# Where the last image's gathers, stores and loads stand in the order of a four-layer hybrid kernel

## The chip, the cores and the metric

The kernel runs on one core of a Trainium2 chip, in one launch. The metric is the device time of the whole kernel in microseconds, the median of several runs. The engines are named as in the profile: PE is the matrix engine, DVE the vector engine, ACT the scalar engine, POOL the general engine, and SP the engine that here issues nearly all DMAs. Each engine works through its own instructions in the order in which they were issued to it and waits on semaphores for what the others produce. SP does so too: a DMA issue that has to wait holds up every issue behind it.

## The reference

Four images of 32 x 32 positions with 256 channels (1024 tokens each) pass four layers. Cut to what matters:

```python
# layer 0: ln -> w_in -> 3x3 depthwise conv -> gelu -> selective scan, 512 channels, 64 states
h = dA * h + (dtt * xt)[:, :, None] * Bt[:, None, :]        # 1024 steps
y = einsum('bdn,bn->bd', h, Ct)                             # ... + skip, ln, w_out, residual
# layer 1: grouped convolutions; layer 2: masked attention and a mixture of 8 experts
# layer 3: selective scan, 512 channels, 16 states
dt = softplus(x_conv @ W_dt + b_dt)
y_t = (h_new * C_t[:, None, :]).sum(-1)                     # ... * silu(gate) @ W_out, residual
# layer 3's mixture: every token is given to its two best of 8 experts
h = gelu(xf @ w1[e] + bb1[e]); y = h @ w2[e] + bb2[e]; out = out + cw[:, e:e+1] * y
```

## The kernel before

**Scans.** There are eight selective scans, one for each image of layer 0 and of layer 3, in the order `SCANS` = (0,0), (0,1), (3,0), (0,2), (3,1), (0,3), (3,2), (3,3). Each is cut into units of 128 pairs of channel and state by 1024 steps: 256 units for a scan of layer 0, 64 for one of layer 3, 1280 in all. For one unit SP loads `dA<-dt` (512 KB, line 501, four units ahead, five buffers), ACT takes the exponential, PE spreads the input's three bf16 parts over the states (`ps_rep`), DVE multiplies by the rows of B and runs the scan instruction, POOL multiplies `h` by the rows of C, and PE sums the states (`ps_y`). The outputs go by ACT (`yo`) and SP (line 552) to memory and are read back (`y_back`, line 924).

**Ticks.** All other work is written as generators (`front`, `middle` and `last` for each image), and one step of a generator is a tick. `run()` issues, after each half of a unit, up to `TICKS` = 2 ticks, and only while no engine's planned clock is ahead of the vector engine's. So the order on every engine is fixed when the kernel is built: units and ticks woven together. `pipe(items, step1, step2, ...)` is a software pipeline: in one tick it issues the last step of an old item first and the first step of the newest last. `need()` forces ticks where a scan's inputs are not yet made; a new chunk of parts may be late by `LATEST` = 5 units. `beside(main, other)` alternates the ticks of two generators; `some(other, n)` takes n ticks of another; `until(name, b)` yields empty ticks until a mark is set in `passed`, while the order is made.

**Startup.** `prepare()` runs the preparation parts one after the other; the last, `prepare_moe`, clears 4 MB of memory for the piles with 15 stores of 256 KB (line 1616) over five ticks. `front(1)` follows, which loads image 1 (line 791, 1 MB), takes its layer norm (`ln_st`), and puts it through `w_in` and the depthwise convolution (`inward`).

**Layer 3's front.** `front3` makes a scan's inputs. `steps` computes dt and its product with the input, and splits that in three bf16 parts: `project` (PE, then ACT's softplus), `add` (DVE, POOL), `split` (stores dt, line 698; ACT casts part 0; DVE takes the remainder; ACT casts part 1), `low` (part 2), `store` (line 713). For image 3 (`last`) the first two items are done ahead, with `BETWEEN` = 8 ticks of image 2's piles in between (`self.other`), and the later items alternate with those piles.

**Experts.** `piles` does layer 3's mixture for one image. Its tokens have been scattered by expert (POOL, indirect DMA) into 15 piles of 256 rows. Items go through a pipeline: `t` loads a pile's rows (`fetch`, line 1909) and turns them on PE (`ps_gx`) with a copy by ACT; two `h` items multiply by W1 with a gelu; an `o` item multiplies by W2 (`ps_e`), and a copy `x` (ACT for image 2, DVE for image 3, `lone`) is stored to `results` (line 1974). `layer(0, t)` and `layer(1, t)` load W1 and W2 of a pile's expert (line 1915), two buffers each. Rows have `many` buffers: 3 for image 2, 8 for image 3. At the end `gather` brings back each token's two rows (POOL, indirect DMA, `rows_m<-results,slot`), `add` adds them with their shares (DVE, `tb_rows`), and the image goes out (line 2009). Image 2's piles lie beside scan (3,3), the last one; image 3's come after all scans.

Almost all engine instructions are recorded at line 135, that of a helper, so the views are read by tile names.

Of the kernel before, what the change touches and what calls it, by code (L numbers as in the profile page):

```python
# [9 lines left out]
F32 = mybir.dt.float32  # L10
BF16 = mybir.dt.bfloat16
# [7 lines left out]
P = 128  # L19
NB = 4  # L20
L = 1024
TB = L // P
C = 256
# [6 lines left out]
FEW = 256  # L30
PILES = (2 * L + NEXP * (FEW - 1)) // FEW
# [18 lines left out]
BETWEEN = 8  # L50
# [93 lines left out]
END = object()  # L144


class Hybrid:
# [503 lines left out]

    def steps(self, fp, key, w, src, chunks, bias, u, between=None):


        nc = self.nc
# [5 lines left out]
        def tile2(tag, bufs):  # L663
            return fp.tile([P, 512], F32, tag="sp_" + tag, name="sp_" + tag, bufs=bufs)

        def linear(item):
            d, g = item
            ps = self.ps("ps_dt")
            self.mm(ps, lambda k: w(k, d), src, chunks, slice(g * 512, (g + 1) * 512))

            r, e, l = (tile2(t, n) for t, n in (("r", 3), ("e", 2), ("l", 3)))
            nc.scalar.activation(r, ps, AF.Relu, bias=bias[:, d : d + 1])
            nc.scalar.activation(e, ps, AF.Abs, bias=bias[:, d : d + 1])
            got[item] = r, e, ps, l
# [17 lines left out]
            by.tensor_tensor(r, l, r, ALU.add)  # L692
            by.tensor_tensor(l, r, u[:, d, g * 512 : (g + 1) * 512], ALU.mult)

        def split(item):
            d, g = item
            r, _, _, x = got[item]
            nc.sync.dma_start(self.mem["dt", *key, d][:, g * 512 : (g + 1) * 512], r)
            X = fp.tile([P, 3, 512], BF16, tag="parts", name="parts", bufs=3)
            rest = tile2("x", 2)  # L700
            nc.scalar.copy(X[:, 0, :], x)
            nc.vector.tensor_tensor(rest, x, X[:, 0, :], ALU.subtract)
            nc.scalar.copy(X[:, 1, :], rest)
            got[item] = rest, X

        def low(item, by=nc.gpsimd):
            rest, X = got[item]
# [12 lines left out]
        if between is not None:  # L720
# [16 lines left out]
            self.parts_direct(range(1), nc.scalar)  # L737
            self.ready.add(("parts", *key, 0))
            yield 3.0
        yield from self.pipe(items, project, add, split, low, store, cost=3.0)  # L740

# [33 lines left out]
    def front(self, b):  # L777
# [3 lines left out]
        with tc.tile_pool(name=f"f{b}", bufs=1, side="right") as op:  # L781
# [4 lines left out]
            with tc.tile_pool(name=f"fa{b}", bufs=1, side="right") as fp:  # L786
# [9 lines left out]
                pads = [fp.tile([P, 34, 34], F32, name=f"pad{i}") for i in range(2 + len(vector))]  # L796
                for pad in pads:
                    nc.gpsimd.memset(pad, 0.0)
                yield 1.0
                xT = fp.tile([P, 2, L], F32, name="xT0")  # L800
                if b:
# [22 lines left out]

                def inward(item):
                    d, g, k = item
                    pad = pads[2 + vector.index(d) if d in vector else d % 2]
                    if g < 0:
                        h = k
# [752 lines left out]
    def prepare_moe(self, st):  # L1582

        nc, a = self.nc, self.a
        self.router, self.b2, raws = {}, {}, {}
        for which, router, b2 in (
            (2, "L2_ffn_router_w", "L2_ffn_b2"), (3, "L3_ffn_gate_w", "L3_ffn_b2")
        ):
            wr = self.const.tile([P, 2, NEXP], F32, name=f"wr{which}")
            if a[router].shape[0] == NEXP:  # L1590
                raws[which] = st.tile([NEXP, C], F32, name=f"raw{which}")
                nc.sync.dma_start(raws[which], a[router])
            else:
                nc.sync.dma_start(wr, a[router].rearrange("(k p) e -> p k e", p=P))
            self.router[which] = wr
            self.b2[which] = self.const.tile([NEXP, C], F32, name=f"b2{which}")
            nc.sync.dma_start(self.b2[which], a[b2])
        self.gb = self.const.tile([P, NEXP], F32, name="gb")
        nc.sync.dma_start(
            self.gb, a["L3_ffn_gate_b"].rearrange("(o e) -> o e", o=1).to_broadcast([P, NEXP])  # L1600
        )
        self.bout3 = self.rows("L3_attn_b_out")
        self.earlier = self.const.tile([P, P], BF16, name="earlier")
        make_upper_triangular(nc, self.earlier, diag=False)
        count = st.tile([P, PILES], I32, name="counti")
        nc.gpsimd.iota(count, pattern=[[1, PILES]], base=0, channel_multiplier=0)
        self.count = self.const.tile([P, PILES], F32, name="count")
        self.one8 = self.const.tile([P, NEXP], F32, name="one8")
        zeros = st.tile([P, 2, C], F32, name="zeros")
        nc.gpsimd.memset(zeros, 0.0)  # L1610
        self.piled = self.keep(("piled",), [PILES * FEW, C])
        yield
        nc.vector.tensor_copy(self.count, count)
        nc.vector.memset(self.one8, 1.0)
        for t in range(PILES):
            nc.sync.dma_start(self.pile(self.piled, t), zeros)
            if t % 3 == 2:
                yield
        for which, raw in raws.items():
            ps = self.ps("ps_r", (P, C))  # L1620
            for k in range(2):
                nc.tensor.transpose(
                    ps[:, k * NEXP : (k + 1) * NEXP], raw[:, k * P : (k + 1) * P],
                    self.ident[:NEXP, :NEXP],
                )
            nc.vector.tensor_copy(
                self.router[which].rearrange("p k e -> p (k e)"), ps[:, : 2 * NEXP]
            )
# [267 lines left out]
    def piles(self, op, b, tb, picks, slot, share, whose, bias):  # L1896
# [2 lines left out]
        w1, w2 = self.a["L3_ffn_W1"], self.a["L3_ffn_W2"]  # L1899
        results = self.keep(("results", b), [PILES * FEW, C])  # L1900
        lone = b == NB - 1
        many = 8 if lone else 3
        reuse = self.x0.rearrange("p (k j) c -> p k j c", k=4)
        rows, weights, turned, hidden, got = {}, {}, {}, {}, {}

# [14 lines left out]
        def one(item):  # L1920
            kind, t, i = item
            if kind == "t":
                x = rows.pop(t)
                got[item] = ps = self.ps("ps_gx", (P, 2, FEW))
                for c in range(2):
# [24 lines left out]
        def two(item):  # L1950
# [7 lines left out]
            elif kind == "h":  # L1958
                ps = got.pop(item)
                for k in range(2):  # L1960
# [1 line left out]
                    nc.scalar.activation(  # L1962
                        hidden[t][:, f, :], ps[:, k, :], AF.Gelu, bias=bias[:, t, f : f + 1]
                    )
                if i == 1:
                    layer(0, t + 2)
            else:
                y = reuse[:, 2 + t % 2]
                ps = got.pop(item)
# [1 line left out]
                    nc.vector.tensor_copy(y, ps)  # L1971
                else:
                    nc.scalar.copy(y, ps)
                nc.sync.dma_start(self.pile(results, t), y)
                layer(1, t + 2)

        items = []
# [11 lines left out]
        for t in range(2):  # L1989
            fetch(t)  # L1990
        yield 0.5
        yield from self.pipe(items, one, two, cost=2.0)

        def gather(j):
            got[j] = x = op.tile([P, 2, C], F32, tag="rows", name="rows_m", bufs=many)
# [12 lines left out]
                )  # L2008
            nc.sync.dma_start(self.image(self.out, b)[:, j, :], tb[:, j, :])

        yield from self.pipe(range(TB), gather, lambda j: None, add, cost=2.0)

    def route(self, gp, lg, cw, renorm, spots=None):

# [53 lines left out]
    def front3(self, b, tb):  # L2068
# [3 lines left out]
        with tc.tile_pool(name=f"g{b}", bufs=1, side="right") as op:  # L2072
# [76 lines left out]
            with tc.tile_pool(name=f"gc{b}", bufs=1, side="right") as fp:  # L2149
# [6 lines left out]
                def low(g):  # L2156
# [2 lines left out]
                    self.mm(ps[: 2 * N, :], lambda k: w_bc[:, k, :], u, DC, cols)  # L2159
                    nc.scalar.activation(bct[:, cols], ps[: 2 * N, :], AF.Identity, bias=bbc)  # L2160

                yield from self.pipe(range(2), low, cost=3.4)
                nc.sync.dma_start(self.keep(("bc", *key), [2 * N, L]), bct)
                steps = self.steps(
                    fp, key, lambda k, d: w_dt[:, k, d * P : (d + 1) * P], u, DC,
                    vec["L3_attn_b_dt"], u, self.some(self.other, BETWEEN) if last else None,
                )
                if last:
                    steps = self.beside(steps, self.other, lambda: ("parts", *key, 0) in self.ready)
# [107 lines left out]
    def prepare(self):  # L2277
        with self.tc.tile_pool(name="prepb", bufs=1, side="right") as st:
# [6 lines left out]
                yield 0.5  # L2285
            for part in parts:
                for _ in part:
                    yield 1.0
                yield 3.0

    def middle(self, b):
# [56 lines left out]

    def last(self, b):
        if b == NB - 2:  # L2350
            self.other, before = self.ahead(b + 1, "right"), self.other
            yield from self.beside(before, self.other)
            return
        if b == NB - 1:
            for more in self.other:
                if more is not END:
                    yield more
            return
        with self.tc.tile_pool(name=f"e{b}", bufs=1, side="right") as tp:
            tb = tp.tile([P, TB, C], F32, name="tb")  # L2360
# [47 lines left out]
```

## Time and profile before

| | us |
|---|---|
| median of 3 runs (lowest to highest) | 6268.16 (6258.17 to 6272.56) |
| the profiled execution | 6287.39 |
| its span | 6285.6 |
| DVE busy | 5033.5 (80%) |
| PE busy | 4983.6 (79%) |
| POOL busy | 3891.1 (62%) |
| ACT busy | 3391.2 (54%) |

The profile is of one execution, on one core. The span is from the first recorded instruction to the last; 1.8 us of the execution lie around it. The page gives each engine's busy time and the span in 40 equal slices, where a digit is the busy share in tenths and one slice is 157 us. `PEclk` is the granted clock of the matrix engine (mean 0.823). A line of the timeline gives start, duration, engine, line, operation and tiles, the number of instructions drawn together, and in brackets the engine's idle time before it with what ended it. A line of the waits gives who waited for what, the sum, the count and the longest. A row of the windows gives, for one stretch, the busy time of each engine with its instructions, the granted clock, the mean busy share of the 16 DMA engines and GB/s.

### The profile page before, as it was taken

How to read it: one execution, taken by the hardware profiler on the slowest of the kernel's cores; microseconds unless marked ns; L12 is line 12 of the kernel's file. 1: busy time of each engine (PE TensorE's matmuls, PEld its weight loads, DVE VectorE, ACT ScalarE, POOL GpSimd, SP SyncE). 2: the span in 40 equal slices, each digit the busy share in tenths (PEclk: the TensorE clock that was granted, in tenths of full speed). 3: DMA queues.
4: the chain of work that ended last, by engine and by line, in shares of the span. 5: the costliest groups of instructions: out<-in, count | busy, mean ns of one | idle time of the engine just before them, and what ended most of it. 6: DMA issues, size and time to landing. Idle time of an engine off the chain costs nothing. (4 is left out here: it accounts for less than half of the span.)

```text
span 6285.6 us, 59857 instructions
## 1 busy us (share of the span) xinstructions
PE 4983.6 (79%) x19881; PEld 2042.3 (32%) x19881; DVE 5033.5 (80%) x3977; ACT 3391.2 (54%) x4329; POOL 3891.1 (62%) x2016
## 2 busy tenths in 40 slices
PE   5686776579898567979869978979769969996757
PEld 2121221032243112225324532234225432453436
DVE  5889898998898998889899988889889984224661
ACT  3465665345577434649647735558637734425622
POOL 2787768665576866568676766568767754114551
PEclk7686786589899658979869988979869979998868
DMA  3554555544345556435555576345555673025945
GB/s 108 180 155 161 164 176 181 174 147 129 116 161 179 189 160 165 141 121 173 175 191 166 182 181 166 125 131 185 161 183 176 186 183 96 12 70 150 246 109 171
DMA packets 382814, 977.72 MB, mean 156 GB/s; under 512 B 40644, under 2 KB 149520, under 8 KB 380880
## 3 DMA queue, kind: packets, MB, share of 16 engines
q1 hardware_dynamic: 376704, 962.73, 50.8%
q0 software_dynamic: 5200, 10.53, 0.6%
q8 instruction: 163, 2.67, 0.2%
q14 instruction: 171, 1.40, 0.1%
q10 hardware_dynamic: 576, 0.39, 0.0%
HBM read 867.76 MB, written 108.36 MB: 155 GB/s over the span
## 5 line engine op out<-in xcount | busy, mean ns | idle before, releaser
L135 POOL TENSOR_TENSOR h<-h,rows 128x1024 f32<-128x1024 f32 x1280 | 3025.0, 2367 | 1706.8 <-DVE h L135 1324.9
L135 DVE TENSOR_TENSOR_SCAN h<-dA,ps_rep 128x1024 f32<-128x1024 f32 x1280 | 2924.4, 2285 | 212.7 <-ACT dA L135 82.2
L135 DVE TENSOR_TENSOR ps_rep<-ps_rep,rows 128x1024 f32<-128x1024 f32 x1280 | 1549.3, 1210 | 189.6 <-PE ps_rep L135 188.3
L135 PE MATMUL ps_rep<-S,spread_L_conv_A_log 96*128 96x512 bf16 x2048 | 753.4, 457 | 778.8 <-DVE h L135 733.2
L135 ACT ACTIVATE dA<-dA,A_L_conv_A_log 128x1024 f32<-128x1024 f32 x1024 | 1125.7, 1142 | 440.3 <-DMA dA<-dt 405.3
L135 PE MATMUL ps_y<-h,collect_L_conv_A_log 128*32 128x512 f32 x4096 | 706.6, 745 | 17.2 <-POOL h L135 17.2
L135 PEld LDWEIGHTS <-spread_L_conv_A_log 96*128 96x128 bf16 x2048 | 160.0, 103 | 1566.9 <-DVE h L135 1272.8
L135 PE MATMUL ps_e<-we,h_m 128*128 128x256 f32 x2528 | 587.7, 383 | 5.5 <-ACT h_m L135 5.5
L135 ACT ACT_TABLE_LOAD x395 | 506.8, 1283 | 30.9 <-DMA dA<-dt 14.7
L135 PEld LDWEIGHTS ps_e<-we,h_m 128*128 128x128 f32 x2528 | 478.8, 191 | 129.6 <-ACT h_m L135 25.8
L135 PE MATMUL ps_h<-xTm,we 128*128 128x512 f32 x1024 | 487.9, 607 | 0.1
L135 ACT ACTIVATE p<-ps_sc 128x512 f32<-128x512 f32 x404 | 219.3, 594 | 331.6 <-PE ps_sc L135 327.7
L135 ACT ACTIVATE dA<-dA,A_L_attn_A_log 128x1024 f32<-128x1024 f32 x256 | 284.3, 1144 | 194.7 <-DMA dA<-dt 162.1
L135 PE MATMUL ps_rep<-S,spread_L_attn_A_log 96*128 96x512 bf16 x512 | 182.0, 443 | 194.0 <-DVE h L135 171.8
L135 PE MATMUL ps_at<-p,v 128*32 128x512 f32 x1024 | 275.0, 617 | 0.2 <-ACT p L135 0.2
L135 PE MATMUL ps_at<-p,ones 128*32 128x512 f32 x1024 | 275.0, 617 | 0.0
L135 ACT ACTIVATE h_m<-ps_h,cols 128x512 f32<-128x512 f32 x256 | 171.0, 686 | 186.8 <-PE ps_h L135 185.0
L135 PEld LDWEIGHTS ps_h<-xTm,we 128*128 128x128 f32 x1024 | 192.4, 193 | 218.7 <-issue 154.1
L135 PE MATMUL ps_sc<-qT,kT 32*128 32x512 f32 x808 | 249.0, 666 | 5.9 <-ACT p L135 2.0
L135 PE MATMUL ps_cv<-pad,diag 128*128 128x512 f32 x504 | 231.0, 599 | 0.0
L135 PEld LDWEIGHTS ps_y<-h,collect_L_conv_A_log 128*32 128x32 f32 x4096 | 93.7, 118 | 339.5 <-issue 227.7
L135 POOL TENSOR_TENSOR tb<-tb,y_m 128x512 f32<-128x512 f32 x160 | 202.7, 1274 | 0.0
(392 smaller groups left out, 5609.5 us busy)
## 6 DMA issues: line engine op xcount, KB each, us to landing
dA<-dt SPq DMA_DIRECT2D x1280, 512.0 KB
we<-in_L_ffn_W_dram SPq DMA_DIRECT2D x92, 512.0 KB
parts<-parts SPq DMA_DIRECT2D x60, 384.0 KB
S<-parts SPq DMA_DIRECT2D x90, 256.0 KB
dt<-sp_r SPq DMA_DIRECT2D x64, 256.0 KB
y<-yo SPq DMA_DIRECT2D x128, 128.0 KB
y_back<-y SPq DMA_DIRECT2D x64, 256.0 KB
we<-in_L_ffn_w_dram SPq DMA_DIRECT2D x64, 256.0 KB
```

The source lines that it names most:

```text
L135: return got(*args, **kw)
```

## The change

Five things are moved or split; what is computed stays the same.

- The memory for the piles is cleared in `front(1)`: one of the 15 stores, from a tile `empty` made there, ahead of each of the first 15 `inward` items. The five ticks in `prepare_moe` go, and the other parts' `yield` in `prepare` becomes `pass` (none of them has a tick left there).
- `piles` has a third step, `three`: the loads of W1 and W2 for pile t+2 and the store of a result are issued one tick later, for both images.
- Image 2's rows have 2 buffers instead of 3; its gathers and adds follow each other without an empty tick.
- Image 2's gathers wait, in the order of issue, until image 3's piles have begun (`turned`, set at the `t` item of pile 1). For that, image 3's `last` also runs what is left of image 2.
- For image 3, `steps` splits the parts in two ticks, `high` and `remainder` (`apart`), with four buffers instead of three for `l` and the parts; and one tick of image 2's piles (its first weights and rows) is taken ahead of the pipe of `low` in `front3`.

```diff
--- before.py
+++ after.py
@@ -651,7 +651,7 @@
-    def steps(self, fp, key, w, src, chunks, bias, u, between=None):
+    def steps(self, fp, key, w, src, chunks, bias, u, between=None, apart=False):
         nc = self.nc
@@ -668,7 +668,7 @@
             ps = self.ps("ps_dt")
             self.mm(ps, lambda k: w(k, d), src, chunks, slice(g * 512, (g + 1) * 512))
-            r, e, l = (tile2(t, n) for t, n in (("r", 3), ("e", 2), ("l", 3)))
+            r, e, l = (tile2(t, n) for t, n in (("r", 3), ("e", 2), ("l", 3 + apart)))
             nc.scalar.activation(r, ps, AF.Relu, bias=bias[:, d : d + 1])
             nc.scalar.activation(e, ps, AF.Abs, bias=bias[:, d : d + 1])
             got[item] = r, e, ps, l
@@ -692,16 +692,24 @@
             by.tensor_tensor(r, l, r, ALU.add)
             by.tensor_tensor(l, r, u[:, d, g * 512 : (g + 1) * 512], ALU.mult)
-        def split(item):
+        def high(item):
             d, g = item
             r, _, _, x = got[item]
             nc.sync.dma_start(self.mem["dt", *key, d][:, g * 512 : (g + 1) * 512], r)
-            X = fp.tile([P, 3, 512], BF16, tag="parts", name="parts", bufs=3)
+            X = fp.tile([P, 3, 512], BF16, tag="parts", name="parts", bufs=3 + apart)
+            nc.scalar.copy(X[:, 0, :], x)
+            got[item] = x, X
+
+        def remainder(item):
+            x, X = got[item]
             rest = tile2("x", 2)
-            nc.scalar.copy(X[:, 0, :], x)
             nc.vector.tensor_tensor(rest, x, X[:, 0, :], ALU.subtract)
             nc.scalar.copy(X[:, 1, :], rest)
             got[item] = rest, X
+
+        def split(item):
+            high(item)
+            remainder(item)
         def low(item, by=nc.gpsimd):
             rest, X = got[item]
@@ -737,7 +745,8 @@
             self.parts_direct(range(1), nc.scalar)
             self.ready.add(("parts", *key, 0))
             yield 3.0
-        yield from self.pipe(items, project, add, split, low, store, cost=3.0)
+        parted = (high, remainder) if apart else (split,)
+        yield from self.pipe(items, project, add, *parted, low, store, cost=3.0)
@@ -796,6 +805,12 @@
                 pads = [fp.tile([P, 34, 34], F32, name=f"pad{i}") for i in range(2 + len(vector))]
                 for pad in pads:
                     nc.gpsimd.memset(pad, 0.0)
+                empty = None
+                if b == 1:
+                    self.piled = self.keep(("piled",), [PILES * FEW, C])
+                    empty = fp.tile([P, 2, C], F32, name="empty")
+                    nc.gpsimd.memset(empty, 0.0)
+                    piles = iter(range(PILES))
                 yield 1.0
                 xT = fp.tile([P, 2, L], F32, name="xT0")
                 if b:
@@ -824,6 +839,8 @@
                 def inward(item):
                     d, g, k = item
+                    if empty is not None and (t := next(piles, None)) is not None:
+                        nc.sync.dma_start(self.pile(self.piled, t), empty)
                     pad = pads[2 + vector.index(d) if d in vector else d % 2]
                     if g < 0:
                         h = k
@@ -1606,16 +1623,9 @@
         nc.gpsimd.iota(count, pattern=[[1, PILES]], base=0, channel_multiplier=0)
         self.count = self.const.tile([P, PILES], F32, name="count")
         self.one8 = self.const.tile([P, NEXP], F32, name="one8")
-        zeros = st.tile([P, 2, C], F32, name="zeros")
-        nc.gpsimd.memset(zeros, 0.0)
-        self.piled = self.keep(("piled",), [PILES * FEW, C])
         yield
         nc.vector.tensor_copy(self.count, count)
         nc.vector.memset(self.one8, 1.0)
-        for t in range(PILES):
-            nc.sync.dma_start(self.pile(self.piled, t), zeros)
-            if t % 3 == 2:
-                yield
         for which, raw in raws.items():
             ps = self.ps("ps_r", (P, C))
             for k in range(2):
@@ -1899,7 +1909,7 @@
         w1, w2 = self.a["L3_ffn_W1"], self.a["L3_ffn_W2"]
         results = self.keep(("results", b), [PILES * FEW, C])
         lone = b == NB - 1
-        many = 8 if lone else 3
+        many = 8 if lone else 2
         reuse = self.x0.rearrange("p (k j) c -> p k j c", k=4)
         rows, weights, turned, hidden, got = {}, {}, {}, {}, {}
@@ -1920,6 +1930,8 @@
         def one(item):
             kind, t, i = item
             if kind == "t":
+                if lone and t == 1:
+                    self.passed.add(("turned", b))
                 x = rows.pop(t)
                 got[item] = ps = self.ps("ps_gx", (P, 2, FEW))
                 for c in range(2):
@@ -1962,8 +1974,6 @@
                     nc.scalar.activation(
                         hidden[t][:, f, :], ps[:, k, :], AF.Gelu, bias=bias[:, t, f : f + 1]
                     )
-                if i == 1:
-                    layer(0, t + 2)
             else:
                 y = reuse[:, 2 + t % 2]
                 ps = got.pop(item)
@@ -1971,7 +1981,14 @@
                     nc.vector.tensor_copy(y, ps)
                 else:
                     nc.scalar.copy(y, ps)
-                nc.sync.dma_start(self.pile(results, t), y)
+                got[item] = y
+
+        def three(item):
+            kind, t, i = item
+            if kind == "h" and i == 1:
+                layer(0, t + 2)
+            if kind == "o":
+                nc.sync.dma_start(self.pile(results, t), got.pop(item))
                 layer(1, t + 2)
         items = []
@@ -1989,7 +2006,9 @@
         for t in range(2):
             fetch(t)
         yield 0.5
-        yield from self.pipe(items, one, two, cost=2.0)
+        yield from self.pipe(items, one, two, three, cost=2.0)
+        if not lone:
+            yield from self.until("turned", NB - 1)
         def gather(j):
             got[j] = x = op.tile([P, 2, C], F32, tag="rows", name="rows_m", bufs=many)
@@ -2008,7 +2027,8 @@
                 )
             nc.sync.dma_start(self.image(self.out, b)[:, j, :], tb[:, j, :])
-        yield from self.pipe(range(TB), gather, lambda j: None, add, cost=2.0)
+        between = (lambda j: None,) if lone else ()
+        yield from self.pipe(range(TB), gather, *between, add, cost=2.0)
     def route(self, gp, lg, cw, renorm, spots=None):
@@ -2159,11 +2179,13 @@
                     self.mm(ps[: 2 * N, :], lambda k: w_bc[:, k, :], u, DC, cols)
                     nc.scalar.activation(bct[:, cols], ps[: 2 * N, :], AF.Identity, bias=bbc)
+                if last:
+                    yield from self.some(self.other, 1)
                 yield from self.pipe(range(2), low, cost=3.4)
                 nc.sync.dma_start(self.keep(("bc", *key), [2 * N, L]), bct)
                 steps = self.steps(
                     fp, key, lambda k, d: w_dt[:, k, d * P : (d + 1) * P], u, DC,
-                    vec["L3_attn_b_dt"], u, self.some(self.other, BETWEEN) if last else None,
+                    vec["L3_attn_b_dt"], u, self.some(self.other, BETWEEN) if last else None, last,
                 )
                 if last:
                     steps = self.beside(steps, self.other, lambda: ("parts", *key, 0) in self.ready)
@@ -2285,7 +2307,7 @@
                 yield 0.5
             for part in parts:
                 for _ in part:
-                    yield 1.0
+                    pass
                 yield 3.0
     def middle(self, b):
@@ -2348,13 +2370,12 @@
     def last(self, b):
         if b == NB - 2:
-            self.other, before = self.ahead(b + 1, "right"), self.other
+            after = self.ahead(b + 1, "right")
+            self.other, before = (more for more in after if more is not END), self.other
             yield from self.beside(before, self.other)
             return
         if b == NB - 1:
-            for more in self.other:
-                if more is not END:
-                    yield more
+            yield from self.other
             return
         with self.tc.tile_pool(name=f"e{b}", bufs=1, side="right") as tp:
             tb = tp.tile([P, TB, C], F32, name="tb")
```

## The prediction

> **What bounds the kernel now.** I read the page's slices first, then busy time by stretch, then the timeline and the waits of the places where the change acts.
>
> ```profile
> span 6285.6 us, 59857 instructions
> ...
> DVE  5889898998898998889899988889889984224661
> ...
> L135 DVE TENSOR_TENSOR_SCAN h<-dA,ps_rep 128x1024 f32<-128x1024 f32 x1280 | 2924.4, 2285 | 212.7 <-ACT dA L135 82.2
> L135 DVE TENSOR_TENSOR ps_rep<-ps_rep,rows 128x1024 f32<-128x1024 f32 x1280 | 1549.3, 1210 | 189.6 <-PE ps_rep L135 188.3
> ```
>
> For 33 of the 40 slices DVE is at 8 or 9 tenths. It does 1280 scan units, each a multiply (1.21 us) and a scan (2.29 us); the timeline repeats them every 3.54 us. Everything else is woven beside them, so up to the last scan only what stops DVE counts. After it (the 4224661) the tail is a chain of its own. The stretches where the change acts:
>
> ```profile
> core 0: us, PE busy (x) PEld busy (x) DVE busy (x) ACT busy (x) POOL busy (x), PEclk, DMA share, GB/s
> 240.00:262.00 22.00, 4.52 (x15) 0.72 (x13) 9.92 (x15) 2.43 (x2) 11.57 (x8) 0.58 0.89 287
> 5720.00:5830.00 110.00, 75.47 (x250) 37.18 (x248) 71.17 (x50) 68.86 (x90) 72.98 (x43) 0.81 0.65 176
> 5830.00:6007.00 177.00, 137.38 (x628) 87.34 (x632) 130.32 (x77) 115.93 (x142) 96.89 (x45) 0.88 1.02 251
> 6007.00:6048.00 41.00, 15.81 (x44) 1.62 (x36) 37.96 (x26) 6.11 (x6) 33.05 (x24) 0.50 0.44 122
> 6130.00:6254.00 124.00, 113.46 (x540) 99.13 (x540) 10.38 (x15) 35.04 (x76) 0.00 (x0) 0.94 0.57 188
> ```
>
> First row, startup: DVE idle more than half the time, DMA nearly full. Second and third, image 3's scan while image 2's expert piles run: DVE idle 39 of 110 and 47 of 177 us, with DMA full (1.02) in the latter. Fourth, the last scans: DVE full, but with the wrong work. Fifth, image 3's own piles: PE bound, DVE and POOL free.
>
> **The change part by part.** The sum is made against the profiled execution (6287.39 us, span 6285.6), 19 us above the median of 6268.16; I take the difference over to the median unchanged.
>
> *Zero rows.*
>
> ```profile
> 236.35 2.15 SPq L1616 DMA_DIRECT2D piled<-zeros  x3
> 239.91 9.96 SPq L1616 DMA_DIRECT2D piled<-zeros  x12
> 253.95 0.42 SPq L791 DMA_DIRECT2D x<-in_x_dram  x1
> 261.37 0.43 DVE L135 BATCH_NORM_STATS2 ln_st<-x 128x6 f32<-128x256 f32 x1 [11.69 <-DMA dA<-dt]
> ```
>
> Fifteen stores (256 KB each, 4 MB) hold SP until 249.9. Behind them queue dA loads and image 1's 1 MB x load, which goes out at 253.95; DVE stands 11.69 us for it (the releaser printed is a dA load, but the statistics read x). The change takes the stores and five ticks out here, so front 1 starts about one unit (3.5 us) earlier in the order, and the x load goes out at about 243 and lands about 7 us later as now (253.95 to 261.37), near 250. DVE gets to the statistics one unit earlier, at about 246, so it stalls some 4 us instead of 11.69: gain 7 (3 to 10, the lower end if dA loads still hold it). The stores come back one for each `inward` item (0.2 to 0.7 us of SP each in the rows above) at about 280 to 340, where the share is 0.50 at 153 GB/s: hidden there at nothing; uncovered they cost 15 x 0.7 = 10. The memset (522 ns on POOL) only moves. The Trainium skill, "DMA: Bandwidth & Descriptors", section "Issuing engines are not separate DMA queues", speaks against a gain: it says that all DMAs share the same 16 engines and interleave, so moved bytes cost what they cost; by it alone 4 MB would only move its 16 us (4 MB at the 251 GB/s above), and the sum would lose these 7. I stay with the share of 0.50.
>
> *Image 3's parts and the early tick.* Five weights and rows (2.5 MB) go out about 30 us sooner, into a stretch with a share of 0.10 (5640 to 5680). First loads now go at 5682.08 and the rows land at 5692.3, but ACT's softplus runs to 5693.25 anyway, so PE starts piles only 0.5 us sooner. The eight ticks between reach one tick further: one 4.8-us o item and a gelu (0.84 + 1.28 of table load). Then PE stands 7.43 us for the first rep, which takes the o item; ACT loses 2 us, under its 11.1-us wait for dA. The waits of 5690 to 5800 show what the split into two ticks is for:
>
> ```profile
> DVE sp_x L135 <- ACT parts L135: 25.2, 6, 6.7
> ACT parts L135 <- DVE sp_x L135: 4.5, 6, 0.8
> ```
>
> DVE, in order, stands 4.2 us six times at the subtract behind ACT's cast, holding its units. With a tick between, the cast is done when the subtract comes: 25 us of this wait go. But the stretch is a loop of ACT and PE (projection 5.2 on PE, then 6.6 on ACT: 11.8 of a cycle of about 12, from the relu times 5744.1, 5756.6, 5768.6, 5780.5, 5794.5), so what comes next for DVE is ps_rep or dA; only ACT's own 4.5 us and no more leave the loop. The added tick makes the second parts ready later, against a limit of 5 units: a forced tick, 0 to +4. Net -3 (bounds -25, if DVE's wait were the whole loop, weakly supported; +4): I use -8 to +3.
>
> *Piles a tick later.* In 5800 to 6010 SP, in order, stands behind:
>
> ```profile
> SPq L1974 <- ACT x L135: 39.2, 10, 9.0
> SPq L501 <- DMA we<-in_L_ffn_W_dram: 6.4, 5, 2.0
> ```
>
> Ten results stores issued in the tick of their copy hold SP 39.2 us, and behind each are dA loads. A tick later the copy is done; these waits should go. But 5830 to 6007 moves 44.4 MB at 251 GB/s with a share of 1.02: the queue is not empty while SP stands, and 177 us is the bytes. I book 0 (-15 if a third of 39.2 was empty time). Against it stand two row buffers for three: the fetch of t+2, in the same tick as ACT's copy, now waits for PE's transposes of t itself, not t-1. Before, this was 1.2 us once. The fetch has dA loads and y stores behind it on SP; PE may trail by an o item (3.6), a y (1.07) and a rep (0.6), so 0 to 5.3 us for each of 13. The dA loads run four units (14 us) ahead and hide one such wait: 0, upper end in the rival below. Of image 3's piles later weights have about 11 us to spare at 7.35 us a pile: 0.
>
> *Gathers of image 2.* 16 gathers and 16 adds leave the last scans:
>
> ```profile
> 6006.91 2.29 DVE L135 TENSOR_TENSOR_SCAN h<-dA,ps_rep 128x1024 f32<-128x1024 f32 x1
> ...
> 6013.15 4.86 DVE L135 SCALAR_TENSOR_TENSOR tb_rows<-rows_m,share,tb_rows 128x256 f32<-128x256 f32 x2 [2.83 <-DMA rows_m<-results,slot]
> 6017.92 2.28 DVE L135 TENSOR_TENSOR_SCAN h<-dA,ps_rep 128x1024 f32<-128x1024 f32 x1
> ...
> 6045.38 2.28 DVE L135 TENSOR_TENSOR_SCAN h<-dA,ps_rep 128x1024 f32<-128x1024 f32 x1
> ```
>
> From 6006.91 to 6045.38 are 7 units in 38.47 us; at the pace before, 7 x 3.54 = 24.8. Gain 13.7, and nothing else is late: DMA share is 0.44, POOL's h is 2.35 of 3.54. The chain behind the last scan (h, y, ACT, store, y_back 3.58 us, ps_o) is unchanged. The gathers now start behind image 3's scatters, which end at 6126.3; POOL then idles 130.78 us to 6257. The condition that holds them back acts in the order of issue alone; no engine waits. 16 x 1.31 us of issue, adds of 0.48 as in the last gathers: with two buffers a gather waits for the add two before it, about 2.9 us for each of 8, done near 6155; behind it on POOL is nothing before 6257. Eight out stores (0.33 us of SP each) stand ahead of the results stores and weights of piles 0 and 1: within the 11 us to spare. But their 3 MB meet image 3's first 3 MB, for which PE stands 27.68 us (share 0.74 in 6126 to 6140): 2 to 3 MB of it at 251 GB/s shared is up to 6 on the first rows. I take +3 (0 to 6), all on the path, as PE paces this stretch.
>
> **Sum.** -7 - 3 + 0 - 13.7 + 3 = -20.7: span about 6265, execution 6266.7, and median 6268.16 - 20.7 = 6247.
>
> **The rivals.** *Slower: the two row buffers.* Thirteen fetches stand on SP for PE, each with dA loads behind it while DMA is full, so lost SP time isn't caught up. At 3 us a pile that is 39, net -20.7 + 39 = +18: 6286. It decides from 21/13 = 1.6 us a pile reaching the scan. For it: PE busy 137 of 177 us, and dA waits in every second unit; against: four dA loads ahead, and 39.2 us of other stalls freed on the same queue. *Gains that only move:* zeros meet the first part of front 1 (startup 3 instead of 7), the first part gives 0, contention 6, and of the 13.7 some 3 come back as SP stalls: -3 - 0 + 6 - 10.7 = -8, 6260. For it: the share of 0.89 with which startup is full anyway. *Faster still:* the freed 39.2 us let dA land sooner, -15 more: 6232. Against: the share of 1.02. *The change doesn't do what it says* for the gathers (they stay beside units because the condition is met early): -7 - 3 = -10, 6258; the scatters precede it on POOL, so I give it little and count it with the second rival.
>
> **How the numbers follow.** Forecast 0.52 (6247), only moved 0.22 (6260), slower 0.15 (6286), faster still 0.11 (6232). This kernel's measurement tells about 0.2% (12.5 us) from no change: below 6255.6 is faster, above 6280.7 slower. Of the forecast 0.48 lies under 6255.6 and 0.04 within the bound (startup 3 and first part +3 together), of the moved case 0.04 under and 0.18 within, of the slower one 0.01 within: faster 0.48 + 0.11 + 0.04 = 0.63, same 0.04 + 0.18 + 0.01 = 0.23, slower 0.14. The forecast's own range is 6247 with startup ±4, first part -5/+6, saturated -8 (about half of its end), contention ±3: 6230 to 6259. Eight in ten take in the moved case and most of the faster one; left out are the slower case but for its lower end, and the lower end of the faster one, together just under 0.2: 6225 to 6278.
>
> **What would show it.** Right: DVE idle of about 4 us ahead of the first ln_st near 250, not 11.69; zero stores near 280 to 340; the last eight scans every 3.54 us; POOL's first gathers near 6127 and a first PE transposition of image 3's piles at most 6 us later relative to the scatters; SP's 39.2 us gone at the results store. Wrong: `SPq L1909 <- PE ps_gx` grown from 1.2 us to tens, dA waits on ACT in 5830 to 6007 grown with it; a stretch from the first image 3 unit to the last longer than now; piles of image 3 slower than 7.35 us each.

## The result, and the profile after

The changed kernel takes 6241.55 us (median of 7 runs, 6228.52 to 6266.49) against 6268.16 (7 runs, 6258.17 to 6280.55): a ratio of 0.9968, 95% interval 0.9954 to 0.9982, or 11 to 29 us. (The ratio and its interval are those given with the comparison; the quotient of the two medians is 0.9958.) The forecast was 6247. Run once more beside three other kernels it gave 0.9962 (0.9949 to 0.9975). Its profiled execution took 6266.49 us, again one of the slower ones of its kernel.

The page after, same places as before:

```profile
span 6264.7 us, 59864 instructions
...
DVE  5889898998898998889899988889889985233751
...
L135 DVE TENSOR_TENSOR_SCAN h<-dA,ps_rep 128x1024 f32<-128x1024 f32 x1280 | 2923.9, 2284 | 212.3 <-ACT dA L135 81.4
L135 DVE TENSOR_TENSOR ps_rep<-ps_rep,rows 128x1024 f32<-128x1024 f32 x1280 | 1551.9, 1212 | 215.4 <-PE ps_rep L135 214.4
```

Nothing shows at this scale: the same instructions at the same lengths, and the sum of waits over the whole span is no smaller. The stretches say more (engines, then granted clock, DMA share, GB/s; the fourth runs from unit 1272 to just behind the start of the last scan, that of before from one unit later):

```profile
core 0: us, PE busy (x) PEld busy (x) DVE busy (x) ACT busy (x) POOL busy (x), PEclk, DMA share, GB/s
240.00:262.00 22.00, 6.98 (x24) 2.10 (x20) 18.17 (x26) 2.43 (x2) 10.80 (x8) 0.58 0.43 141
5720.00:5830.00 110.00, 81.90 (x290) 44.82 (x290) 78.84 (x51) 79.49 (x104) 74.37 (x43) 0.83 0.76 202
5830.00:6007.00 177.00, 132.66 (x582) 79.89 (x581) 133.63 (x79) 105.81 (x129) 101.20 (x48) 0.85 0.96 245
6000.00:6027.00 27.00, 15.59 (x47) 1.91 (x46) 25.94 (x16) 7.15 (x7) 18.13 (x8) 0.55 0.36 92
6110.00:6234.00 124.00, 112.14 (x540) 98.20 (x540) 17.45 (x30) 34.98 (x76) 12.34 (x13) 0.95 0.64 209
```

At startup DVE is busy 18.17 us instead of 9.92 and the DMA share is halved. Some 3 of the 18 us are no work: a cast of 128 x 15 (`count`) that takes 0.14 us before now lasts 3.25, to 248.8, which is when POOL's fills of `pad` and `empty` end. Image 3's units have 79 us of DVE work in the second stretch instead of 71. In the last row DVE and POOL now hold the moved gathers and adds; PE is as busy as before.

**One clock for all profiles.** A span is a poor measure here, since two executions of one kernel differ by 20 us. Instead I take from the timeline the start of each of the 1280 scan instructions, numbered 0 to 1279, and compare how long stretches of units take. DVE's order of work is the same in both kernels for nearly all units from 40 to 1200. Image 3's layer-3 scan is units 1216 to 1279. In us:

| stretch | before | before, again | after | after, again |
|---|---|---|---|---|
| units 21 to 36 (startup stall) | 77.8 | 76.8 | 69.7 | 70.6 |
| 36 to 60 | 92.5 | 92.1 | 95.7 | 97.1 |
| 60 to 1215 | 4856.5 | 4835.9 | 4863.3 | 4846.1 |
| 1215 to 1216 (image 3's attention, experts, front) | 452.9 | 452.1 | 454.8 | 454.2 |
| 1216 to 1272 | 286.6 | 288.2 | 276.7 | 279.9 |
| 1272 to 1279 (the gathers of before) | 42.0 | 43.0 | 24.8 | 24.8 |
| 1279 to the end of the span | 240.2 | 238.4 | 239.5 | 239.1 |

The third row is most of the span and differs by 20 us between two executions of the kernel before. So the row says nothing of the change, and a single profile can't be read by its length. The largest change is in the row of the gathers. Its two ends in the kernel after, units 1272 and 1279 (before, they start at 6003.37 and 6045.38):

```profile
6000.43 2.29 DVE L135 TENSOR_TENSOR_SCAN h<-dA,ps_rep 128x1024 f32<-128x1024 f32 x1
...
6025.23 2.29 DVE L135 TENSOR_TENSOR_SCAN h<-dA,ps_rep 128x1024 f32<-128x1024 f32 x1
```

### The profile page after: what moved, and what is told of

It reads as the page before. It is cut to its first block, busy times and chain, and to the rows that moved or that the text cites. A ratio compares the mean times of both kernels' runs of the same rounds, so it can differ in the third digit from the quotient of the medians.

```text
span 6264.7 us, 59864 instructions
## 1 busy us (share of the span) xinstructions
PE 4989.5 (80%) x19881; PEld 2046.6 (33%) x19881; DVE 5023.5 (80%) x3977; ACT 3387.2 (54%) x4328; POOL 3891.9 (62%) x2016
## 5 line engine op out<-in xcount | busy, mean ns | idle before, releaser
L135 PE MATMUL ps_at<-p,v 128*32 128x512 f32 x1024 | 276.7, 621 | 0.2 <-ACT p L135 0.2
L135 PE MATMUL ps_at<-p,ones 128*32 128x512 f32 x1024 | 276.7, 621 | 0.0
```

The source lines that it names most:

```text
L135: return got(*args, **kw)
```

## The experiments

The theory: the gain is the stall at startup and, above all, the gathers; the later stores and weights bring nothing, since the DMA engines are full there. The rivals: the gain lies in the freed SP time, or is partly given back.

**The kernel before, again.** No edit.

> The kernel before, once more, to see how far two executions of one kernel differ in each stage. All theories expect ratio 1.000. If the start times of its units wander by 5 to 10 us against the first profile between units 40 and 1200 (as those of the kernel after do, where DVE's order of work is the same), that wandering is no effect of the change; if they agree within 2 us, the change must have an effect there that was not seen.

Ratio 1.0007 (0.9995 to 1.0019). Its units stand 16 to 22 us ahead of those of the first profile from unit 520 on, though the kernel is the same. The wandering is of executions, and the table above is what can be compared.

**The gathers alone.**

```diff
+        if not lone:
+            yield from self.until("turned", NB - 1)
...
-        yield from self.pipe(range(TB), gather, lambda j: None, add, cost=2.0)
+        between = (lambda j: None,) if lone else ()
+        yield from self.pipe(range(TB), gather, *between, add, cost=2.0)
```

(with the mark `turned` and the two edits of `last`)

> The kernel before with image 2's gathers behind the last scan and nothing else of the change. Theory (the gathers are most of the gain): from the scan of unit 1272 to that of unit 1279 (the last) it takes 7 x 3.54 = 24.8 us as in the kernel after, not 42.0 as before, and the time from the last scan to the end stays at 240 us: about 17 us faster than before, ratio near 0.9973. Rival (the gain is the freed SP and startup, and the moved gathers only press on image 3's first loads): the 17 us at the scans come back as a longer stretch from the last scan to the end (250 us or more), net under 7 us, ratio 0.999 or more.

Ratio 0.9962 (0.9948 to 0.9976). Units 1272 to 1279 take 24.8 us, and the time from the last scan to the end is 239.8. The 17 us are there and don't come back.

**The zero rows alone.**

```diff
-        for t in range(PILES):
-            nc.sync.dma_start(self.pile(self.piled, t), zeros)
-            if t % 3 == 2:
-                yield
...
+                    if empty is not None and (t := next(piles, None)) is not None:
+                        nc.sync.dma_start(self.pile(self.piled, t), empty)
```

> The kernel before with only the zero rows' stores moved into the second front. Theory: DVE's stall ahead of the first statistics of image 1 falls from 11.7 to about 3.6 us, unit 36 starts 4.9 us sooner than before, and nothing after it gives that back by its order of work: 5 us faster, ratio 0.9992. Rival 1 (the gain is taken back at the next wait of the order, or lost to the stores in the second front): unit 36 again 4.9 us sooner, unit 120 not, ratio 1.000. Rival 2 (the stores' 4 MB cost their 16 us among the loads of the second front): slower by up to 10 us, ratio up to 1.0016.

Ratio 0.9984 (0.9972 to 0.9995). Units 21 to 36 take 69.0 us (77.8 and 76.8 in the kernel before), units 36 to 60 take 95.7 (92.5 and 92.1). Over all ten profiles with the moved zeros, the first stretch is 68.6 to 71.1 and the second 95.7 to 97.9; over the four without, 76.7 to 78.4 and 91.5 to 92.6. So 7.6 us are gained and 4.5 of them come back at once: both theory and first rival are half right. DVE's extra waits there are for `ps_rep` and dA (9.2 and 1.1 us instead of 7.0 and 0). The stores' bytes are not what does it. Thirteen of the fifteen stores go out in units 26 to 38, and these take 43.4 to 45.0 us in the ten profiles and 44.0 to 45.3 in the four. The loss lies behind them: units 38 to 50 take 47.1 to 49.8 us instead of 42.5, with DVE waiting mostly for PE; from 332 to 362 us here PE is busy 29.4 of 30 us, at a DMA share of 0.44. That leaves the order shifted by five ticks as the likely cause; which work of PE is in the way wasn't tested.

**All but the gathers.** The kernel after, with the four edits of the gathers undone.

> The kernel after with image 2's gathers left where they were before, beside the last units. Theory: the last seven units take 42 us again; of the gain some 17 us are gone, what is left is the 5 us of startup and whatever the piles and parts bring: ratio to before near 0.9990 (0.998 to 1.000). Rival (SP's freed stalls are the gain): ratio still near 0.997, since SP's waits at the results store stay at about 11 us instead of 39 without the moved gathers.

Ratio 0.9999 (0.9984 to 1.0013): the rival falls, SP's waits at the results store are 14.2 us in units 1216 to 1272 (50.4 before), and no gain is left. It is even less than expected, and DVE's timeline shows why:

```profile
5983.94 1.00 DVE L135 SCALAR_TENSOR_TENSOR tb_rows<-rows_m,share,tb_rows 128x256 f32<-128x256 f32 x2 [7.13 <-DMA rows_m<-results,slot]
5991.72 6.40 DVE L135 SCALAR_TENSOR_TENSOR tb_rows<-rows_m,share,tb_rows 128x256 f32<-128x256 f32 x2
6001.35 2.59 DVE L135 SCALAR_TENSOR_TENSOR tb_rows<-rows_m,share,tb_rows 128x256 f32<-128x256 f32 x2
```

Here the gathers among the units cost more than before: from unit 1266 to 1279 it takes 78.3 us, against 64.6 before and 47.4 to 51.1 in the kernels with moved gathers. Part of that is only place: all 16 adds lie ahead of the last scan here, and four lay behind it before. Part is that with two row buffers POOL's gathers now wait for the adds (1.08 us, five times), and the pace of the units beside them is 5.83 us instead of 5.49. That the two buffers are the whole of the rest is likely, but wasn't separated from the other parts. The gain of the two-tick parts is there all the same: units 1216 to 1248 take 170.4 us, against 180.0 to 189.1 in all kernels without them.

**Gathers and zeros together.** Both edits above.

> The kernel before with the moved gathers and the moved zero rows only; piles, buffers and parts as before. By the runs so far the two parts alone gave 24 and 10 us (ratios 0.9962 and 0.9984). Theory (they add up, and the other three parts cost time): 28 to 34 us faster than before, ratio 0.9945 to 0.9955, faster than the kernel after (0.9968). Rival (the other parts are worth some 5 to 13 us in the last scan, as one profile of the kernel after shows, 276.7 us from unit 1216 to 1272 against 287 to 291 in four others): slower than the kernel after, ratio 0.9975 to 0.998.

Ratio 1.0004 (0.9991 to 1.0016), where two parts had given 24 and 10 us. SP's timeline beside image 3's first loads:

```profile
6117.77 19.59 SPq L1916 DMA_DIRECT2D we<-in_L_ffn_W_dram  x4
```

Four issues in 19.6 us, with many of SP's own register instructions at about 0.7 us (medians of 0.02 to 0.27 in the kernel after), while POOL issues the gathers; PE's first rows come 11 us late, and from the last scan to the end it takes 251.8 us. This kernel and three described below (later stores and weights, two buffers, late adds) ran on another chip than the runs above, and image 3's attention, experts and front (unit 1215 to 1216) also take 457.5 to 462.9 us in all four profiles, against 450.8 to 458.0 in the ten others. The same kernel on a third chip:

> Moved gathers and moved zero rows only, once more. In its first profile SP took 19.6 us for the four weight issues that take 3.9 us elsewhere (each of its instructions about 0.7 us, while POOL issued the moved gathers back to back), and from the last scan to the end it took 252 us instead of 240. Theory (a clash of SP's issue with POOL's gathers, which this kernel always has): again 10 us or more from last scan to first rows beyond the 89 us of the kernel after, ratio 0.9985 or more. Rival (it was that chip, or that execution): SP's four issues in about 4 us, 240 us from the last scan to the end, ratio 0.995 to 0.997.

```profile
6098.06 3.95 SPq L1916 DMA_DIRECT2D we<-in_L_ffn_W_dram  x4
```

Ratio 0.9980 (0.9971 to 0.9989), SP's four issues in 3.95 us, 239.3 us from the last scan to the end. So the slow issue is no property of the kernel alone: the rival holds in that. Nor is it one of that chip alone: there the kernel with late adds, whose gathers don't lie beside these four issues, takes 3.88 us for them. Yet it isn't the forecast's 28 to 34 us either, but 7 to 18.

**Later stores and weights; then two buffers.** On the same chip as the 19.6 us issue above.

```diff
+        def three(item):
+            kind, t, i = item
+            if kind == "h" and i == 1:
+                layer(0, t + 2)
+            if kind == "o":
+                nc.sync.dma_start(self.pile(results, t), got.pop(item))
+                layer(1, t + 2)
...
-        many = 8 if lone else 3
+        many = 8 if lone else 2
```

(the first hunk in both, the second in the second kernel alone)

> The same with the piles' stores and weights a tick later too, image 2's rows still in three buffers. Theory (a later issue on SP brings nothing where the DMA engines are full): SP's waits at the results store fall from 39 to about 11 us, yet units 1216 to 1272 take 287 to 291 us as in the kernel before, and the ratio is that of the gathers and zeros alone within 0.0015. Rival (freed SP time lets dA land sooner): units 1216 to 1272 in under 280 us, 8 to 15 us faster than the gathers and zeros alone.

> The kernel after with image 3's parts as before (no second tick for them, no early tick of the piles): against the run before it only the rows of image 2 have two buffers instead of three. Theory (a fetch with two buffers holds SP behind PE's transposes, but four dA loads lie ahead): SP's wait for the transposes grows from about 1 us to 10 to 40 us, units 1216 to 1272 take at most 3 us more than with three buffers. Rival (every such wait reaches the scan): 15 to 39 us more in that stretch, ratio 0.998 or more.

Ratios 0.9998 (0.9983 to 1.0012) and 0.9986 (0.9974 to 0.9998). SP's waits at the results store fall from 50 to 26.6 and 26.8 us in units 1216 to 1272, not to 11; the stretch takes 291.3 and 288.1 us, in the span of 286.6 to 292.1 of the other profiles without the two-tick parts. Where the time freed on SP goes is seen in SP's waits, here the kernel with gathers and zeros on the same chip, then the one with later stores:

```profile
SPq L1977 <- ACT x L135: 53.2, 12, 10.7
SPq L501 <- DVE h L135: 51.8, 17, 9.6
```

```profile
SPq L501 <- DVE h L135: 76.3, 23, 10.9
...
SPq L1982 <- ACT x L135: 26.6, 8, 8.1
```

Of the 26.6 us no longer spent at the results store, 24.5 are spent waiting for DVE's scans at the dA loads of line 501, where the five dA buffers come free. The loads were as far ahead as the buffers let them be, so an earlier SP brings nothing. Of the slow rival (fetches that hold SP) nothing is seen: among SP's longer waits of that stretch there is none for PE's transposes.

**Where the gathers' cost lay.** Gathers where they were, adds behind image 3's scatters:

```diff
+            yield from self.pipe(range(TB), gather, cost=2.0)
+            yield from self.until("turned", NB - 1)
+            yield from self.pipe(range(TB), add, cost=2.0)
```

> The kernel before with image 2's gathers where they were, beside the last units, landing in the used-up weight buffers, and only the 16 adds and the out stores behind image 3's scatters. What in the gathers cost the 17 us: DVE's adds (2.3 us a unit, and a stop of 11 us at the first), or POOL's issue (two of about 1.3 us a unit beside a multiply of 2.35, 4.95 us for a pace of 3.54). Theory (DVE's adds): units 1272 to 1279 in 24.8 to 27 us, all of the 17 us gone, ratio near 0.997. Rival (POOL's issue): the units at 4.9 to 5.5 us each, or POOL's multiplies 8 to 10 us behind the last scan, so that 8 to 17 us remain; ratio 0.9985 or more.

Units 1272 to 1279 take 28.3 us, although POOL still issues the gathers between its multiplies. POOL's view around the last scan (6022.13), and the adds alone on DVE:

```profile
6022.63 4.65 POOL L135 TENSOR_TENSOR h<-h,rows 128x1024 f32<-128x1024 f32 x2
6027.44 1.05 POOL L135 DMA_INDIRECT rows_m<-results,slot  x1 [0.16 <-issue]
6028.79 1.01 POOL L135 DMA_INDIRECT rows_m<-results,slot  x1 [0.30 <-issue]
6029.82 2.35 POOL L135 TENSOR_TENSOR h<-h,rows 128x1024 f32<-128x1024 f32 x1
```

```profile
6094.97 6.49 DVE L135 SCALAR_TENSOR_TENSOR tb_rows<-rows_m,share,tb_rows 128x256 f32<-128x256 f32 x14
```

So 13.7 of the 17.2 us leave the scans with the adds on DVE: 0.46 us each here, 2.27 for two beside POOL's multiplies before. But POOL's last multiply ends at 6032.2, 10 us behind the start of the last scan (4.8 in the kernel after), and from that start to the end of the span it takes 245.1 us, 5 to 6 more. With the 3.5 us left at the scans, about 9 of the 17 us remain, now as POOL's issues: the rival's second form has come about, and the theory (all of the 17 us gone) holds for only half. The adds set the pace before, 5.49 us a unit, with POOL's two issues and a multiply close behind at some 4.95; only both together, moved away, bring the 17 us. The ratio, 0.9998 (0.9988 to 1.0008) on the chip with the slow front, shows no gain.

**The whole change again, and the gathers in POOL's gap.** The second puts the gathers ahead of image 3's scatters, into the weights' used-up buffers, and the adds into DVE's wait for the router:

```diff
-            yield from self.until("turned", NB - 1)
+            yield from self.until("gated", NB - 1)
...
+            yield from self.pipe(range(TB), gather, cost=2.0)
+            yield from self.until("lg", NB - 1)
+            for j in range(TB):
+                add(j)
```

(`gated` is marked behind image 3's last gate product, `lg` behind its router's product)

> The kernel after, once more, on the same chip as the three others of this call. The runs so far do not add up: the gathers alone 0.9962, the zeros alone 0.9984, both together 1.0004, the whole change 0.9968, but not all on one chip. Theory (the change's gain is the gathers' 17 us and the startup's 7, whatever else is in it): ratio 0.996 to 0.9975. Rival (the gain of the first comparison was of that chip, or luck): ratio 0.998 or more.

> The kernel after, but image 2's gathers are issued ahead of image 3's scatters, in the 42.9 us in which POOL waits for the slots, landing in the used-up weight buffers; the 16 adds stand in DVE's 13 us wait for the router's product. Theory (nothing then meets SP's first loads of image 3): units at 3.54 us to the end as in the kernel after, 238 to 240 us from the last scan to the end, SP's four weight issues in 4 us on any chip: as fast as the kernel after where that has no clash (ratio to before 0.996 to 0.997), 10 us faster where it has. Rival (the gathers stand in the way of the chain to the slots): 5 to 10 us more from the last scan to the end.

> The same placing of the gathers on the kernel before with the moved zero rows, without the later stores and weights and without the two-tick parts. Theory (those three parts are worth nothing in sum): within 0.0015 of the run before it. Rival 1 (they are worth 5 to 13 us in the last scan): 0.002 slower, with units 1216 to 1272 in 287 to 291 us against 277 to 282. Rival 2 (they cost time, as the difference of the zeros alone, 0.9984, and all but the gathers, 0.9999, says): 0.0015 faster or more.

The whole change gave 0.9962 (0.9949 to 0.9975, median 6245.54), so its rival (the first gain was of that chip, or luck) falls; with the gap it gave 0.9962 (0.9948 to 0.9976, median 6237.80, 5 runs), and with the gap but without the parts and the piles 0.9979 (0.9970 to 0.9988). The gap works as laid out,

```profile
6031.91 7.41 DVE L135 SCALAR_TENSOR_TENSOR tb_rows<-rows_m,share,tb_rows 128x256 f32<-128x256 f32 x16
```

and the time from the last scan to the end is 237.8 and 237.2 us, the shortest of all profiles: 1 to 2 us, too little for the times to tell. In both pairs of this chip the kernel without parts and piles is slower by about 0.0018 (11 us), with each ratio known to about 0.001; that is rival 1 of the last expectation. The trace has it in units 1216 to 1248: 182.2 us in gathers and zeros, 173.5 in the whole change. DVE's waits there, without the two-tick parts:

```profile
DVE sp_x L135 <- ACT parts L135: 23.9, 6, 6.7
DVE h L135 <- ACT dA L135: 21.2, 6, 5.6
DVE ps_rep L135 <- PE ps_rep L135: 15.5, 6, 7.7
DVE sp_e L135 <- ACT sp_l L135: 4.2, 1, 4.2
```

and with them:

```profile
DVE h L135 <- ACT dA L135: 24.5, 10, 6.9
DVE ps_rep L135 <- PE ps_rep L135: 15.3, 6, 5.4
DVE sp_e L135 <- ACT sp_l L135: 5.7, 5, 2.6
DVE sp_x L135 <- POOL parts L135: 2.2, 1, 2.2
```

The 24 us behind ACT's cast are gone. Some 8 turn up as other waits (1.4 of them at a line not shown), and 5 more go into the subtracts themselves: the six take 9.2 us instead of 4.2, the long ones beside POOL's multiplies. ACT is busy 119.9 of 173.5 us instead of 110.5 of 182.2, PE 133.0 instead of 125.7. From the first to the sixth relu of that front (ACT's `sp_r`) it takes 54.4 us instead of 61.6: a cycle of 10.9 us instead of 12.3. All three profiles with every part and moved gathers have 275.9 to 279.9 us in units 1216 to 1272; all without the two-tick parts 285.3 to 292.1.

## Why the prediction was right, point by point

- **Gathers, right and too small.** Forecast 13.7, measured 17.2 (42.0 to 24.8). The step that failed is a count: from the scan at 6006.91 to that at 6045.38 lie seven scans, but six paces, so the term should have been 38.47 - 6 x 3.54 = 17.2. What cost the time: the kernel with late adds shows DVE's adds and POOL's issues side by side, with about half of the 17 us gone when the adds alone move.
- **Contention at image 3's first loads, right in place.** From POOL's last scatter to PE's first rows it takes 15.3 us after, 13.3 before: 2 us, forecast 3; in the second pair of profiles 13.3 and 12.6. From the last scan to the end it is 239.5 and 239.1 against 240.2 and 238.4, so nothing of it is left there. The bound of 6 was too low for one case: 11 us with the slow issue of SP, which no row of before showed.
- **Startup, right in size at its place, wrong in what follows.** DVE's stall is 3.59 us instead of 11.69:

```profile
249.93 0.41 SPq L800 DMA_DIRECT2D x<-in_x_dram  x1
256.98 0.43 DVE L135 BATCH_NORM_STATS2 ln_st<-x 128x6 f32<-128x256 f32 x1 [3.59 <-DMA dA<-dt]
```

  The load of x went out at 249.93, not 243, and landed in 7 us as forecast; DVE had work that had moved up too, and 3 us in which it stood until POOL's fills ended. Gain 7.6, forecast 7. "Hidden there at nothing" held for the stores: units 26 to 38, beside 13 of them, take no longer than before. The step that failed is that nothing was booked for the order moved up by five ticks: 4.5 us come back by unit 60, behind the stores, mostly as waits for PE. The Trainium skill ("DMA: Bandwidth & Descriptors", section "Issuing engines are not separate DMA queues") says that all DMAs run on the same 16 engines and interleave, from which the prediction drew that moved bytes would take the gain back; the runs don't show that here.
- **The parts in two ticks, wrong.** Forecast 3, measured about 12 in units 1216 to 1272 (277.5 on average against 289.3), with perhaps 2 lost ahead of them (unit 1215 to 1216: 454.2 against 452.6, leaving out the chip of the slow issue and the kernel without the moved gathers, 458.0; without the parts the profiles spread from 450.8 to 454.8). The step that failed is the loop: the prediction took projection on PE and then ACT's work, 11.8 of a cycle of about 12, as its floor, let only ACT's own 4.5 us leave it, and put the lower bound of 25 aside as "weakly supported". With the tick between, the cycle is 10.8 us in the kernel after and 10.9 in its second profile, below that floor (the shortest of each is 8.7), so the two were not strictly one after the other. That DVE's 24 us behind the cast held back work that ACT and PE could have done meanwhile fits their higher busy shares, but is inferred. What the two ticks and the early tick of the piles each bring was not separated.
- **Later stores and weights, right in size:** 0, with SP's waits at the results store halved by them. The reason was given as full DMA; the waits show the freed time going to the dA buffers that DVE still holds. **The slow rival** did not occur in any run.
- **The sum.** By stages the change is worth -7.6 + 4.5 - 17.2 - 11.8 + 1.6 = -30.5 us; the times say -20 and -24, each with 8 or 9 us either way. The rest isn't accounted for: it can hide in units 60 to 1215, where single profiles differ by more, or in the times' own spread. So the forecast of -20.7 is as close as it is partly by luck. The gathers and the parts were worth 3.5 and 7 us more than it said and the contention of 3 was not seen, the startup was worth 4 less, and the stages, summed, give more than the clock shows.

## What to carry to other kernels

Where one engine works through units in a fixed order, date its instructions unit by unit in both traces and compare stretches; spans that wander by 20 us hide gains of 5. An instruction that stands in order behind another engine's answer can cost more than that engine's share of the loop: here 24 us of such waits went, and 9 to 12 us were gained where the prediction let 4.5 count. When one of two engines that work beside each other is relieved, ask how close the other is: the late adds gave only half. Count paces, not instructions, when a stretch is turned into a rate.

## What the runs showed of the hardware

- DVE's add of 128 x 256 takes 0.46 to 0.48 us while POOL issues DMAs or idles, and 2.27 for two while POOL multiplies. The Trainium skill ("SBUF — State Buffer", section "SBUF: two separate sides") says that a DVE operation with two SBUF inputs and a GpSimd operation that reads SBUF lock each other out for a whole instruction; these times agree with it.
- Four weight issues of SP took 19.6 and 20.3 us in two kernels, with many of SP's instructions at about 0.7 us, and 7.5 us in a third with two row buffers, all on one chip and beside POOL's gathers. On that chip without gathers beside them they took 3.88 us, and on two other chips with gathers 3.9 to 4.0. So it takes that chip and the gathers together; the cause stays open.
- In stretches with equal work, executions differ by steps: units 900 to 960 take 275.2 to 275.7, 279.0 to 279.3, or 283.5 us, in kernels with and without the change.
